# Four-layer conditional kernel on one core: layer 1 turned round, and the last queries moved behind the keys

## The chip, the cores and the metric

The kernel runs on one core of a Trainium2 chip. The metric is device time in microseconds (us), the median of several runs. Everything is fp32.

## The reference

`x` has 64 sequences of 64 tokens of width 512. Four layers follow, each with a residual. Which weights, adapter, cache window or subject matrix a sequence uses comes from small integer inputs.

```
x = x + x @ W0[id[b]] + b0[id[b]]                                  # layer 0: one of 16 matrices
x = x + x @ W1.T + s[ad[b]] * (x @ A[ad[b]].T) @ Bm[ad[b]].T       # layer 1: one of 8 rank-16 adapters
q, k, v = x @ Wq.T, x @ Wk.T, x @ Wv.T                             # layer 2: 8 query heads, 4 key heads of 64
q, k = rope(rms(q)), rope(rms(k)); new k, v go into a paged cache at kv_len[b] ...
x = x + softmax(mask(q k^T)) v @ Wo.T                              # window of 256 positions
x = x + out3,  out3[b] = W3[sub[b]]^T x[b] + side[sub[b]]          # layer 3: contracts over the tokens
```

## The kernel before

The 4096 tokens are 32 tiles of 128 (two sequences each), in groups of 1, 1, 2 and seven times 4 tiles. All instructions stand in an order written out by hand, for every engine. The first stage makes layers 0 and 1 and the queries, keys and values; the second makes attention and layer 3.

In the loop of the first stage, the steps of group g+1's layer 0 alternate with the queries and keys of group g, and after the steps stands layer 1 of group g+1.

- **Layer 0** (`layer0`, L479): p0 of one tile, two sequences side by side as two matmuls of 64 token columns each, every sequence with its own matrix W0 of 1 MB. ACT copies p0 to s0 (L484), TensorE turns it (`turn0`, L491), DVE adds it to x1 (L493), which POOL has filled with x plus the bias (`bias0`, L465). The matrices are loaded by SP two steps ahead (`load_pair0`, L455), four buffers.
- **Layer 1** (`layer1`): features on the partitions and tokens along the rows, a whole group at once. px (L501) is the product with all eight adapters' A (8 x 16 = 128 rows); DVE masks it with each sequence's own adapter and scaling to xa (L503). Then, for each of four blocks of 128 output features, ph is four matmuls with w1 (L512) and one with all eight adapters' B (L513), and DVE adds x1 to x2 (L514).
- **Keys and queries**: pk (L550) and pq (L563), then root mean square and rotation (`turned`, L524 to L544) on ACT, DVE and POOL. The query is turned (`turn_q`, L582), copied by ACT and stored to qTd; the new keys and values go to kvd (L557); `keep_x2` turns x2 back to tokens on the partitions (L573) and stores it to x2d.
- **Old keys** (`collect`, L228 to L237): 34 rounds of an indirect gather of 1 MB by POOL into one of three buffers `st` and a store of 1 MB to kvd by SP. From group 3 on, four rounds stand in each layer 1 and one in the third step.
- **Windows** (`windows`, L240 on): small DVE work that finds which rows of kvd each sequence reads; it is cut into pieces (`background`) that stand between the other work.

PSUM has three pools in the first stage: two banks for p0, two for pt, four for the rest. After the last layer 1 (group 9) stand the four key products of its tiles, then their four queries with the turns, then the second stage.

The second stage has its own PSUM pools, a ring of seven banks and one for the projection. Per tile: gathers of key and value rows from kvd by POOL (`load_kv`, L704), query and mask loads, key turns (L770, L776), scores (L789), softmax on DVE and ACT (L797, L801, L813), turns (L822, L826), attention (L836), projection (L859) and layer 3 (L871). The last tile's query stays in SBUF and is turned at the start of this stage (`turn_last`).

Of the kernel before, what the change touches and what calls it, by code (L numbers as in the profile page):

```python
# [23 lines left out]
E = 16  # L24
# [22 lines left out]
GROUPS = [128, 128, 256] + [512] * 7  # L47
NG = len(GROUPS)
T0 = [sum(GROUPS[:g]) for g in range(NG)]
TG = max(GROUPS)  # L50
# [9 lines left out]
def body(ctx: ExitStack, tc: tile.TileContext, a: dict, out: bass.AP):  # L60
# [10 lines left out]

    const = ctx.enter_context(tc.tile_pool(name="const", bufs=1))
# [10 lines left out]
    qlast = const.tile([128, H, HD], F32, name="qlast")  # L83

    wo_p = ctx.enter_context(tc.tile_pool(name="wo", bufs=1))
    wo = wo_p.tile([128, KC, D], F32, name="wo")
    with ExitStack() as pa:

        wp = pa.enter_context(tc.tile_pool(name="wp", bufs=4))
        xp = pa.enter_context(tc.tile_pool(name="xp", bufs=2))  # L90
        op = pa.enter_context(tc.tile_pool(name="op", bufs=3))
        x1p = pa.enter_context(tc.tile_pool(name="x1p", bufs=1))
        wts = pa.enter_context(tc.tile_pool(name="wts", bufs=1))
        su = pa.enter_context(tc.tile_pool(name="su", bufs=1))
        tt = pa.enter_context(tc.tile_pool(name="tt", bufs=1))
        wk = pa.enter_context(tc.tile_pool(name="wk", bufs=2))
        pl0 = pa.enter_context(tc.tile_pool(name="pl0", bufs=2, space=PSUM))
        pt0 = pa.enter_context(tc.tile_pool(name="pt0", bufs=2, space=PSUM))
        pmm = pa.enter_context(tc.tile_pool(name="pmm", bufs=4, space=PSUM))

        def mm(name):
            return pmm.tile([128, 512], F32, tag="mm", name=name)


        pa.enter_context(tc.manual_schedule(
            engines={getattr(mybir.EngineType, e) for e in ("PE", "DVE", "Activation", "Pool", "SP")}
        ))
# [9 lines left out]
        scal = su.tile([128, 1], F32, name="scal")  # L117
        nc.scalar.dma_start(scal, a["scal"])
        gain = su.tile([128, 2, 2, HALF], F32, name="gain")
# [12 lines left out]
        brow = x1p.tile([B, D], F32, name="brow", tag="xa")  # L132
# [5 lines left out]

        w1 = wts.tile([128, KC, D], F32, name="w1")
        aT = wts.tile([128, KC, NA * RANK], F32, name="aT")  # L140
        bmT = wts.tile([128, D], F32, name="bmT")
        wq = wts.tile([128, KC, D], F32, name="wq")
        wkv = wts.tile([128, KC, D], F32, name="wkv")

        def load_weight(t, name):
            nc.sync.dma_start(t, a[name].rearrange("(c p) f -> p c f", p=128))

# [10 lines left out]

        biasT = su.tile([128, KC, B], F32, name="biasT")
        pb = mm("pb")  # L160
        for c in range(KC):
            TE.transpose(pb[:, c * B : (c + 1) * B], brow[:, c * 128 : (c + 1) * 128], ident[:B, :B])
        S.copy(biasT.rearrange("p c b -> p (c b)"), pb[:, : KC * B])

        def scalars():
            V.tensor_scalar(p16, pidx, 4, None, ALU.logical_shift_right)
            V.tensor_copy(p16f, p16)

            V.tensor_scalar(amask, toki[:, 1, :], p16f, scal, ALU.is_equal, ALU.mult)

            V.tensor_scalar(gain, gain, 1.0, None, ALU.add)
            V.tensor_scalar(gain[:, 0], gain[:, 0], SCALE, None, ALU.mult)
            V.tensor_scalar(gsw[:, :, 0, :], gain[:, :, 1, :], -1.0, None, ALU.mult)
            V.tensor_copy(gsw[:, :, 1, :], gain[:, :, 0, :])
            V.memset(epst, EPS)
            V.tensor_tensor(eye2, ident[:, :64], ident[:, 64:], ALU.add)

        p16 = su.tile([128, 1], I32, name="p16")
        p16f = su.tile([128, 1], F32, name="p16f")
        amask = su.tile([128, B], F32, name="amask")  # L180
        gsw = su.tile([128, 2, 2, HALF], F32, name="gsw")
        epst = su.tile([128, 1], F32, name="epst")

        trig = {name: su.tile([128, NT, HALF], F32, name=name) for name in ("sin", "cos")}

        def rotation(lo):

            sh = [128, 8, HALF]
            hi = lo + 8
# [11 lines left out]
            for name, turn, shift in (("sin", 0.0, 0.0), ("cos", 0.25, 0.5 * PI)):  # L201
                ni = tmp("ni", I32)
# [3 lines left out]
                r = trig[name][:, lo:hi]  # L206
# [12 lines left out]

        quart = su.tile([128, JOLD, 2], I32, name="quart")  # L220

        def collect():

            rows, before = BLOCK // 4, None
            for j in range(JOLD):
                for q in range(2):
                    st = op.tile([128, rows * 2 * G * HD], F32, name="st")
                    P.indirect_dma_start(  # L228
                        out=st, out_offset=None, in_=a["kvc"].rearrange("(n r) d -> n (r d)", r=rows),
                        in_offset=bass.IndirectOffsetOnAxis(ap=quart[:, j, q : q + 1], axis=0),  # L230
                    )
                    if before:
                        nc.sync.dma_start(*before)
                    to = kvd[:OLD].rearrange("(p j q r) d -> p j q (r d)", p=128, q=2, r=rows)
                    before = (to[:, j, q], st)
                    yield
            nc.sync.dma_start(*before)  # L237


        def windows():  # L240
# [59 lines left out]

            ns = NW + 2
            diag = su.tile([B, B, ns], F32, name="diag")
# [6 lines left out]
            ps = mm("pst")  # L309
# [31 lines left out]
            valp = su.tile([128, BLOCK, hb, 2], F32, name="valp")  # L341
            cov = su.tile(sh, F32, name="cov")
            tok = su.tile(sh, F32, name="tok")
# [14 lines left out]
            hit = su.tile([128, BLOCK, 2 * hb], F32, name="hit")  # L358
# [58 lines left out]
            for c in range(3):  # L417
                yield
                po = mm("po")
# [15 lines left out]


        xs = {}

        def load_x(g):
            xs[g] = xp.tile([128, KC, TG], F32, name="xt")[:, :, : GROUPS[g]]  # L440
            nc.sync.dma_start(
                xs[g], a["xT"][:, T0[g] : T0[g] + GROUPS[g]].rearrange("(c p) t -> p c t", p=128)
            )

        x1s, x2s, p0s, qrs = {}, {}, {}, {}

        w0s = {}

        def load_pair0(g, k):

            ws = w0s[g, k] = []
            for b in range(T0[g] // T + 2 * k, T0[g] // T + 2 * k + 2):
                w = wp.tile([128, KC, D], F32, name="w")
                r = nc.sync.value_load(tok1[0:1, 0, b : b + 1], min_val=0, max_val=E - 1)
                nc.sync.dma_start(  # L455
                    w, a["W0"][bass.ds(r, 1)].rearrange("a (c p) o -> p (a c) o", p=128)
                )
                ws.append(w)

        def bias0(g):  # L460

            n = GROUPS[g]
            x1 = x1s[g] = x1p.tile([128, KC, TG], F32, name="x1")[:, :, :n]
            for c in range(KC):
                P.tensor_tensor(  # L465
                    x1[:, c, :].rearrange("p (b t) -> p b t", t=T),
                    xs[g][:, c, :].rearrange("p (b t) -> p b t", t=T),
                    bc(biasT[:, c, T0[g] // T : (T0[g] + n) // T, None], [128, n // T, T]),
                    ALU.add,
                )  # L470

        def layer0(g, k):

            ws, xt = w0s.pop((g, k)), xs[g]
            p0 = pl0.tile([128, D], F32, name="p0")
            for c in range(KC):
                for h in range(2):
                    b = 2 * k + h
                    TE.matmul(  # L479
                        p0[h * T : (h + 1) * T, :], xt[:, c, b * T : (b + 1) * T], ws[h][:, c, :],  # L480
                        start=c == 0, stop=c == KC - 1,
                    )
            s0 = x1p.tile([128, D], F32, name="s0", bufs=2)
            S.copy(s0, p0)  # L484
            p0s[g, k] = s0

        def turn0(g, k):
            s0, x1 = p0s.pop((g, k)), x1s[g]
            pt = pt0.tile([128, KC, 128], F32, name="pt")
            for c in range(KC):  # L490
                TE.transpose(pt[:, c, :], s0[:, c * 128 : (c + 1) * 128], ident)  # L491
            xk = x1[:, :, k * 128 : (k + 1) * 128]
            V.tensor_tensor(xk, pt, xk, ALU.add)  # L493

        def layer1(g):
            x1 = x1s.pop(g)
            n = GROUPS[g]
            gb = slice(T0[g] // T, (T0[g] + n) // T)
            px = mm("px")[:, :n]
            for c in range(KC):  # L500
                TE.matmul(px, aT[:, c, :], x1[:, c, :], start=c == 0, stop=c == KC - 1)  # L501
            xa = x1p.tile([128, TG], F32, name="xa")[:, :n]
            V.tensor_tensor(  # L503
                xa.rearrange("p (b t) -> p b t", t=T), px.rearrange("p (b t) -> p b t", t=T),
                bc(amask[:, gb, None], [128, n // T, T]), ALU.mult,
            )
            x2 = x2s[g] = x1p.tile([128, KC, TG], F32, name="x2")[:, :, :n]
            for oc in range(KC):
                ph = mm("ph")[:, :n]
# [468 lines left out]
```

## Time and profile before

| | |
|---|---|
| median of 3 runs | 993.87 us (993.85 to 994.07) |
| the profiled execution | 993.43 us, span 991.5 us |
| mean granted TensorE clock | 0.994 |
| DMA moved | 257.23 MB, mean 259 GB/s |
| first stage's last layer 1 ends | 549.5 us |
| first scores of the second tile start | 599.2 us |

The profile is of one execution. PE is TensorE, DVE VectorE, ACT ScalarE, POOL GpSimd, SP SyncE; "SPq" and "POOLq" are their queues, which issue DMAs. A group of instructions is named by line, engine and output<-input. The chain of waits follows the work that ended last back from the last instruction. "DMA share" is the mean busy share of 16 DMA engines in a stretch.

### The profile page before, as it was taken

The page shows a single profiled execution, that of the slowest core. Times are in us where ns is not written, and L with a number is a line of the kernel's source. Part 1 is how long each engine was busy: PE and PEld are TensorE (multiplying, and loading weights), DVE is VectorE, ACT ScalarE, POOL GpSimd, SP SyncE. Part 2 cuts the span into 40 slices and gives each one's busy share as a digit, 9 for nine tenths or more (in the row PEclk, how much of TensorE's full clock was granted, in tenths as well). Part 3 has the DMA queues.
Part 4 walks back from the last instruction along what each step waited for, and adds up shares of the span by engine and source line. Part 5 has one row for each costly group of instructions (what it writes and reads, how often), then busy time and mean ns, then how long its engine had stood idle before and what let it go on. Part 6 is the DMA issues. An engine that isn't in the chain of part 4 may idle for free.

```text
span 991.5 us, 16856 instructions
## 1 busy us (share of the span) xinstructions
PE 953.4 (96%) x5289; PEld 530.6 (54%) x5289; DVE 642.1 (65%) x1761; ACT 389.0 (39%) x1043; POOL 348.7 (35%) x463
## 2 busy tenths in 40 slices
PE   3989999999999999999999979999999999999997
PEld 1645444444444444444444446766666667776663
DVE  3664556647756766676474468777777777777772
ACT  1111224222122022032121247666666666666662
POOL 1122322333243333333322265444444444444400
PEclk9999999999999999999999999999999999999999
DMA  8954897988989979979957598566666666666611
GB/s 274 345 207 171 314 353 278 371 312 314 361 336 327 377 281 373 357 283 364 360 214 287 226 303 257 180 206 204 207 199 210 204 206 209 204 201 199 209 50 43
DMA packets 115115, 257.23 MB, mean 259 GB/s; under 512 B 22194, under 2 KB 32819, under 8 KB 106323
## 3 DMA queue, kind: packets, MB, share of 16 engines
q1 hardware_dynamic: 95874, 177.29, 49.7%
q0 software_dynamic: 17744, 77.74, 23.6%
q10 hardware_dynamic: 1408, 1.13, 0.4%
q8 instruction: 42, 0.69, 0.3%
q14 instruction: 47, 0.38, 0.1%
HBM read 186.62 MB, written 69.50 MB: 258 GB/s over the span
## 4 chain that ended last, share of the span: by engine, by line
PE 92%; DVE 4%; DMA 2%; ACT 1%; issue 0%; SPq 0%; ACTq 0%; DVEq 0%
PE py L859 12%; PE p L479 12%; PE pk L550 12%; PE pq L563 11%; PE ph L512 10%; PE po L836 8%; PE ps L789 7%; PE ppt L822 6%; PE ph L513 3%; PE pkt L770 2%; PE px L501 2%; PE pz L871 2%; PE pt L491 1%; PE ppt L826 1%; PE pkt L776 1%; PE pqt L582 1%
## 5 line engine op out<-in xcount | busy, mean ns | idle before, releaser
L704 POOL DMA_INDIRECT kv<-kvd,idxn x128 | 126.1, 985 | 184.5 <-PE po L836 138.6
L801 ACT ACTIVATE pr<-pr,mx 128x320 f32<-128x320 f32 x256 | 140.1, 549 | 25.0 <-DVE mx L797 25.0
L797 DVE CUSTOM_DVE_ANT_0 pr<-ps,mb 128x320 f32<-128x320 f32 x256 | 107.9, 487 | 33.6 <-PE ps L789 27.5
L479 PE MATMUL p<-w,xt 128*64 128x512 f32 x512 | 120.1, 608 | 0.1
L859 PE MATMUL py<-wo,oT 128*128 128x512 f32 x256 | 118.4, 605 | 1.6 <-DVE oT L854 0.8
L512 PE MATMUL ph<-x,w 128*128 128x512 f32 (+2 forms) x320 | 118.9, 515 | 0.0
L550 PE MATMUL pk<-wkv,x 128*128 128x512 f32 x256 | 117.5, 604 | 0.0
L563 PE MATMUL pq<-wq,x 128*128 128x512 f32 x256 | 115.2, 592 | 0.0
L484 ACT COPY s<-p 128x512 f32<-128x512 f32 x32 | 18.8, 586 | 187.2 <-PE p L479 187.1
L512 PEld LDWEIGHTS ph<-x,w 128*128 128x128 f32 x320 | 58.1, 196 | 55.2 <-issue 53.6
L813 DVE TENSOR_SCALAR pr<-pr,sm 128x320 f32<-128x320 f32 x256 | 85.1, 394 | 2.3
L550 PEld LDWEIGHTS pk<-wkv,x 128*128 128x128 f32 x256 | 46.3, 189 | 70.6 <-issue 64.7
L836 PE MATMUL po<-pT,kv 128*64 128x128 f32 (+1 forms) x1536 | 82.1, 278 | 0.0
L789 PE MATMUL ps<-kT,qT 64*128 64x320 f32 x512 | 78.7, 447 | 2.5 <-DMA qTd<-qT 2.5
L544 POOL TENSOR_TENSOR qr<-qn,sq 128x512 f32<-128x512 f32 x28 | 46.6, 1665 | 94.4 <-DVE qn L543 77.6
L859 PEld LDWEIGHTS py<-wo,oT 128*128 128x128 f32 x256 | 46.0, 189 | 62.7 <-issue 60.0
L836 PEld LDWEIGHTS po<-pT,kv 128*64 128x64 f32 (+1 forms) x1536 | 68.9, 135 | 19.9 <-DVE mx L797 13.6
L544 POOL TENSOR_TENSOR kvn<-qn,sq 128x256 f32<-128x256 f32 x32 | 23.3, 729 | 158.2 <-ACT kvn L556 132.3
L493 DVE TENSOR_TENSOR x<-pt,x 128x512 f32<-128x512 f32 x32 | 21.9, 691 | 81.2 <-PE pt L491 68.2
L479 PEld LDWEIGHTS p<-w,xt 128*64 128x64 f32 x512 | 35.0, 139 | 67.9 <-issue 65.6
L563 PEld LDWEIGHTS pq<-wq,x 128*128 128x128 f32 x256 | 46.2, 190 | 46.4 <-issue 46.2
L228 POOL DMA_INDIRECT st<-in_kvc,quart x34 | 33.9, 998 | 92.0 <-DMA kvd<-st 86.7
(176 smaller groups left out, 1387.1 us busy)
## 6 DMA issues: line engine op xcount, KB each, us to landing
w<-in_W SPq DMA_DIRECT2D x64, 1024.0 KB
kvd<-st SPq DMA_DIRECT2D x34, 1024.0 KB
kvd<-kvn SPq DMA_DIRECT2D x32, 256.0 KB
x2d<-x2n SPq DMA_DIRECT2D x32, 256.0 KB
x2r<-x2d SPq DMA_DIRECT2D x32, 256.0 KB
qTd<-qT SPq DMA_DIRECT2D x31, 256.0 KB
qT<-qTd SPq DMA_DIRECT2D x29, 256.0 KB
xt<-in_xT SPq DMA_DIRECT2D x7, 1024.0 KB
```

Of the source, the lines that this page charges most:

```text
L479: TE.matmul(p0[h * T : (h + 1) * T, :], xt[:, c, b * T : (b + 1) * T], ws[h][:, c, :], start=c == 0, stop=c == KC - 1,)
L512: TE.matmul(ph, w1[:, c, os_], x1[:, c, :], start=c == 0, stop=False)
L544: X.tensor_tensor(to, qn, t2, ALU.add)
L550: TE.matmul(pk, x2s[g][:, c, ts], wkv[:, c, :], start=c == 0, stop=c == KC - 1)
L563: TE.matmul(pq, x2s[g][:, c, ts], wq[:, c, :], start=c == 0, stop=c == KC - 1)
L704: P.indirect_dma_start(out=kv[:, n, :], out_offset=None, in_=kvd, in_offset=bass.IndirectOffsetOnAxis(ap=at, axis=0),)
L789: TE.matmul(ps[g2][:, :NPOS], qT[rows, gp, b2].rearrange("p h t -> p (h t)"), kT[rows, gp, b2 * NPOS : (b2 + 1) * NPOS], start=True, stop= ...
L797: V.tensor_tensor_reduce(out=p, in0=ps[g2][:, :NPOS], in1=mb[:, b2, :], scale=-1.0, scalar=3.0e38, op0=ALU.add, op1=ALU.min, accum_out=mx[ ...
L801: S.activation(p, p, AF.Exp, bias=mx[:, g, b2 : b2 + 1], scale=-1.0, accum_out=sm[:, g, b2 : b2 + 1],)
L813: V.tensor_scalar(p, p, sm[:, g, b2 : b2 + 1], None, ALU.mult)
L836: TE.matmul(po[b2][g2 * 64 : (g2 + 1) * 64, gp * 128 : (gp + 1) * 128], kv[rows, n, (G + g) * HD : (G + g + 1) * HD], pT[rows, c, m * 128 ...
L859: TE.matmul(py, oT[:, c].rearrange("p b t -> p (b t)"), wo[:, c, :], start=c == 0, stop=c == KC - 1)
```

## The change

Layer 1 holds tokens on the output partitions, as the other products do. For each tile, the weights loaded into TensorE are the tile's x1, the moving operand is w1, and p1 is a tile of 128 tokens by 512 features. Of the adapters, only the two that a tile needs are used. Their A (2 x 16 rows) is loaded per pair of sequences by SP (eight loads of 32 KB for four tiles) and their B is gathered per four tiles by POOL and scaled by DVE. Four tiles stand in the four column groups of 32 for A and in the four row groups of 32 for B. The residual is in w1, to which the identity is added once. ACT copies p1 to x2n, which is stored to x2d as it is and turned once for the products of layer 2.

x is loaded and kept in tiles, not groups, and the bias is added tile by tile. A query stands one step behind its keys. The queries of the last six tiles (26 to 31) stand behind the last layer 1: 26 before the last keys, 27 to 30 between the last keys and the first scores, 31 and the rest of 30 within the first two tiles of attention. Their rotation factors are made before. Old-key rounds are four in each layer 1 from group 3 on and two in the steps (first and second tile of a group). The mask table is made within the pieces of `windows`, and wo is loaded at the start of the second stage. One ring of seven PSUM banks and one for the projection serves both stages.

```diff
-GROUPS = [128, 128, 256] + [512] * 7
+GROUPS = [1, 1, 2] + [4] * 7
+LATE = 6
...
-        pl0 = pa.enter_context(tc.tile_pool(name="pl0", bufs=2, space=PSUM))
-        pt0 = pa.enter_context(tc.tile_pool(name="pt0", bufs=2, space=PSUM))
-        pmm = pa.enter_context(tc.tile_pool(name="pmm", bufs=4, space=PSUM))
+    ring = ctx.enter_context(tc.tile_pool(name="ring", bufs=7, space=PSUM))
+    pyp = ctx.enter_context(tc.tile_pool(name="pyp", bufs=1, space=PSUM))
...
+        def load_a(o):
+            ao = aos[o] = ab.tile([128, 4, 2 * RANK, KC], F32, name="ao")
+            for q in range(8):
+                b = 8 * o + q
+                r = nc.sync.value_load(tok1[0:1, 1, b : b + 1], min_val=0, max_val=NA - 1)
+                nc.sync.dma_start(
+                    ao[:, q // 2, q % 2 * RANK : (q % 2 + 1) * RANK].rearrange("p r c -> p (r c)"),
+                    a["aT"][bass.ds(r, 1)].rearrange("a p f -> p (a f)"),
+                )
...
+        def layer1(tiles):
+            o = tiles[0] // 4
+            ps = slice(32 * (tiles[0] % 4), 32 * (tiles[-1] % 4) + 32)
+            pxa = bank("pxa")
+            for c in range(KC):
+                for i in tiles:
+                    j = i % 4
+                    TE.matmul(pxa[32 * j : 32 * j + 32, :128], aos[o][:, j, :, c], x1s[i][:, c, :], ...)
+            xa = wk.tile([128, 2, T], F32, name="xa", bufs=2)
+            V.tensor_tensor(xa[ps], pxa[ps, :128]..., bc(own2[ps, :, None], ...), ALU.mult)
+            for i in tiles:
+                p1[i] = bank("p1")
+                for c in range(KC):
+                    TE.matmul(p1[i], x1s[i][:, c, :], w1[:, c, :], start=c == 0, stop=False)
+                if i > 3:
+                    next(bg, None)
+                    next(old, None)
+            for i in tiles:
+                js = slice(32 * (i % 4), 32 * (i % 4) + 32)
+                TE.matmul(p1[i], xa[js]..., bos[o][js, :D], start=False, stop=True)
+            for i in tiles:
+                x2n = x2ns[i] = wk.tile([128, D], F32, name="x2n", bufs=4)
+                S.copy(x2n, p1[i])
+                nc.sync.dma_start(x2d[i * 128 : (i + 1) * 128, :], x2n)
...
+            for k in range(m):
+                layer0(i0)
+                load_next(i0)
+                if i0 % 4 == 1 and i0 // 4 + 1 < NT // 4:
+                    load_a(i0 // 4 + 1)
+                    load_b(i0 // 4 + 1)
+                turn_x2(i)
+                pq = product(q, wq, "pq")          # q: the tile before i
+                turn0(i0)
+                run(parts_q(q, pq, P))
+                keep_kv(i, product(i, wkv, "pk"), P)
+                if i > 3 and i % 4 < 2:
+                    next(old, None)
+                turn_q(made.pop(0))                # the tile before q
...
+    for i in range(NT - LATE + 1, NT - 1):         # queries 27 to 30
+        pq = product(i, wq, "pq")
+        if i > NT - LATE + 2:
+            turn_q(i - 2)
+        parts[i] = parts_q(i, pq, V, cs[i])
...
+    keys(0)
```

## The prediction

> **What bounds the kernel now.** The page first: busy times and the chain that ended last.
>
> ```profile
> PE 953.4 (96%) x5289; PEld 530.6 (54%) x5289; DVE 642.1 (65%) x1761; ACT 389.0 (39%) x1043; POOL 348.7 (35%) x463
> ...
> PE 92%; DVE 4%; DMA 2%; ACT 1%; issue 0%; SPq 0%; ACTq 0%; DVEq 0%
> ```
>
> TensorE is the bound nearly everywhere, so PE work removed is time removed, unless something else becomes late. The chain in order of time shows one group of four token tiles (start, us, what; each fp32 matmul shows as two instructions, called passes here):
>
> ```profile
> 253.27 3.44 PE px L501 x8
> 256.71 3.43 PE ph L512 x8
> 260.14 0.86 PE ph L513 x2
> ...
> 273.87 3.58 PE p L479 x16
> 277.46 3.63 PE pk L550 x8
> 281.09 0.44 PE pt L491 x4
> 281.53 3.43 PE pq L563 x8
> ```
>
> Layer 1 lasts from 253.27 to 273.87, 20.60 us: px 3.44, then four times 3.43 + 0.86. The four steps after it take 11.96 each; the group repeats every 68.4. A pass over 512 columns is 0.429 us, a transpose 0.11.
>
> Next, the stretches (span, busy of PE, PEld, DVE, ACT, POOL, granted clock, DMA share, GB/s): two early ones, one layer 1, one whole group.
>
> ```profile
> 70.00:73.00 3.00, 0.95 (x2) 0.84 (x3) 1.89 (x9) 0.00 (x0) 0.00 (x0) 0.73 0.00 0
> 73.00:77.00 4.00, 4.00 (x11) 3.13 (x10) 0.43 (x1) 0.00 (x0) 0.00 (x0) 0.50 0.00 0
> ...
> 253.30:273.90 20.60, 20.60 (x50) 8.76 (x51) 15.18 (x18) 1.32 (x4) 5.23 (x5) 1.00 1.00 371
> 273.90:342.30 68.40, 68.40 (x226) 30.25 (x226) 44.98 (x73) 14.24 (x36) 25.30 (x33) 1.00 0.92 340
> ```
>
> DMA is the second bound: full in layer 1, 0.92 over a group. The timeline shows what each bound already costs (in brackets, the idle time before and its releaser):
>
> ```profile
> 72.05 1.22 PE L513 MATMUL ph<-xa,bmT 128*128 128x256 f32 x2 [3.54 <-DVE xa L503]
> ...
> 342.92 0.94 POOL L228 DMA_INDIRECT st<-in_kvc,quart  x1 [10.74 <-DMA kvd<-st]
> ```
>
> In an early group PE waits for xa, and after that wait runs at clock 0.50. POOL waits 10.7 us for a buffer of old keys, still unharmful.
>
> **Layer 1 on PE.** p1 is 4 matmuls a tile of the same pass: 4 x 3.43 = 13.72 a group. The A products become 16 matmuls of 32 weight columns, 32 passes over 128 tokens. The trace has none four column tiles abreast. Bounds: four quarter-passes of a transpose, 32 x 0.027 = 0.86; nothing abreast, 32 x 0.11 = 3.5. The nearest row has four quadrants abreast:
>
> ```profile
> L836 PE MATMUL po<-pT,kv 64*64 64x128 f32 x512 | 21.4, 282 | 0.0
> ...
> L871 PE MATMUL pz<-x,w 64*64 64x512 f32 x128 | 17.6, 592 | 0.0
> ```
>
> 21.4 / 512 = 42 ns a pass, so 32 x 42 = 1.34. The B products are 8 passes over 512 columns in four row tiles: bounds 8 x 0.107 = 0.86 and 8 x 0.429 = 3.43; the second row gives 137 ns a pass, 1.10. A change of tile shape: pk after the 64-wide p took 3.63 where pq took 3.43, so 0.2 each; three more a group, 0.6. Together 1.34 + 13.72 + 1.10 + 0.6 = 16.76 against 20.60: 3.84 saved, times seven groups 26.9. Ends: 15.44 a group (36 saved) and 21.25 (4.6 lost). The Trainium skill, "TensorEngine Tiling (Array Packing)", section Tiling Modes, says that changing the tiling mode drains TensorE, which speaks against this change; it gives no time, and the 0.2 us above is what the trace shows beside it.
>
> The residual moves into w1 (identity added once): 23 us leave DVE, and one x2 copy per tile (0.6) is added to ACT, 39% busy. Both are hidden under PE. The bias adds are the same POOL work in tile pieces (0.40 each, four a tile), the B scaling adds 8 short DVE operations; nothing of them ends last. x comes in tile pieces of the same bytes. wo is loaded behind the first masks and used by the first projection, two tiles (24 us) later; without that cover its 1 MB is 2.8 us.
>
> **The first three groups.** Gained: xa is now needed only after p1, 3.43 us or more later, so the waits of 2.3 (at 45.4) and 3.5 (at 72.0) go, and with them the half clock, about 2.6 by the stretches; the group of two tiles loses 1.2 of PE work. Lost: where one layer-0 tile is followed at once by its transposes (tiles 2, 4, 6) PE waits for the copy of s0, 0.7 each as at 22.6: 2.1. The eight A loads stand on SP behind w1, x and the second pair of W0, 3.4 MB; at 371 GB/s that is 9.2 us behind the first pair's landing at 16.4, so the first A product starts near 26.5, not 24.1: 2.5 (0 to 10, if the eight small issues themselves hold it). Net 5.9 + 2.6 + 1.2 - 2.1 - 2.5 = 5.1.
>
> **The turn to attention.** Before:
>
> ```profile
> 549.54 13.73 PE pk L550 x32
> ...
> 585.88 6.82 DMA mb<-maskd
> ...
> 599.22 2.35 PE ps L789 x16
> ```
>
> From 549.54 to 599.22 are 49.7 us with about 38 of PE work (4 pk, 4 pq, 9 sets of transposes of 0.43, two key sets, one score set, one turn): some 11.6 of waits, for queries, query and mask loads. Afterwards the keys come first; the last kvn goes out 3.6 us after the last pk, POOL's gathers start 2.8 later as at 570.0, take 6.4 to issue and some 2 to land, 15 in all, and the four products 27 to 30 (13.8) with two transposes (0.9) lie over just that. Masks and queries are issued in the meantime. What is left: 1.1 for the first x2 copy, 0.6 for the queries of tile 30, some 4.5 where normalising tile 0 now shares DVE with two queries. PE work 45.3 (two queries move here out of the loops, 6.9) plus 6.5 is 51.8; less the 6.9 that left the loops, 44.9: 4.8 gained. The shared PSUM ring of seven gives each bank back a full step (12 us) later in the loops, longer than any eviction; if evictions were late it would cost what they lag.
>
> **DMA.** Loads a group before: W0 8, x 1, key/value, x2, q stores 3, and five rounds of old keys (gather 1, store 1): 22 MiB, 23.1 MB; the row says 340 GB/s x 68.4 = 23.3. After: six rounds a group while they last (34 rounds, from layer 1 of group 3 to that of group 8) and 0.5 of adapters: 25.7 MB. PE's period would be 68.4 - 3.8 = 64.6; 340 / 0.92 = 370 GB/s makes 25.7 MB last 69.4. So for five groups DMA falls behind by 4.8 each, 24. W0 is issued two steps ahead (345.9 for use at 366.2) and needs 2.36 MB / 370 = 6.4 to land: 14 us of cover, used up once. Loss 24 - 14 = 10. Bounds: 0, if the full DMA carries a mix with more 8 KB rows faster, and 24, if queueing behind the stores eats the cover. SP also gets 8 adapter loads a group, each with a register load, in the second step: about 1.3 each by the pairs of w3 at 599 to 601, 10 us; it fits in the step, and queued behind it are a kvn store, an old-key store and the next W0, which still has its cover. The Trainium skill, "DMA: Bandwidth & Descriptors", section Specifications, sets 358 GB/s of HBM per core; the layer-1 stretch shows 371, so the measurement decides; by 358 the five groups would fall behind by 36 in place of 24, and the sum below would end at 979.
>
> **Sum.** The profiled run took 993.4 (span 991.5 and 1.9 around it), 0.4 under the median of 993.87. 26.9 + 5.1 + 4.8 - 10 = 26.8 off: 966.6, with the 0.4 put back 967.
>
> **Rivals.** (a) DMA hides: the loops run at 64.6, gain 36.8, 957; with both products at their lower ends 9 less, 948. For it: stores of 8 KB rows, and rounds throttled by POOL, not by W0. Against: share 1.00 in layer 1 already. (b) Slower: POOL is in order, and the bias adds of the next tile now stand in every step behind old-key gathers. The fourth gather of a layer 1 started 21.4 us after that layer's start (321.5 to 342.9); the bias then takes 1.6, and x1's add is due at 16.8 + 7.5 = 24.3. Behind it on DVE stand the queries' and keys' chains, behind those ACT's copy of the next s0, with about 4 us of spare. Every further us is PE's, in six groups; 36.8 / 6 = 6.1 a group turns the whole change into a loss, that is a fourth gather later than 24.3 + 4 + 6.1 - 1.6, +33. For it: DMA slows the very stores it waits for. Against: a slower queue also delays less than half of that, and three buffers stay. At +34.5 it costs 7.6 x 6 = 46, 9 over: 1003. (c) Nothing abreast: layer 1 at 21.25, then 4.6 lost in place of 26.9 gained, and no DMA deficit (period 69): 989. Against: L836 and L871 run abreast.
>
> **Chances.** Forecast with a DMA loss of 3 to 24: 0.50 (955 to 981). (a) 0.30. (b) 0.07. (c) 0.04. The rest, a mixture of lesser waits of POOL and DMA up to 990: 0.09. The range 946 to 985 takes (a) at its lower end and the forecast with the loss of 24 and some waits. Over 0.2% (2 us, about what a measurement of this kernel can tell from no change): faster 0.90, same 0.02, slower 0.08.
>
> **What would show it.** Right: in the chain, a layer 1 of 16 to 17.5 us, 13.7 of it p1; no wait for xa before 82 us and no clock of 0.50 there; DMA share near 1.00 over whole groups 4 to 8, with PE waits for W0 from the second of them on, a few us each; the turn with PE waits of 5 to 8. Wrong: groups of 64 to 65 us throughout (then (a)); PE waiting on s0 or x1 with POOL's bias behind a gather (then (b)); A products above 3 us a group (then (c)).

## The result, and the profile after

The changed kernel takes 1023.61 us (1020.42 to 1025.50) beside 993.86 for the kernel before: 1.0299 times as long, 95% interval 1.0269 to 1.0329. The forecast was 967, range 946 to 985, with 0.90 on faster. Its sign was wrong.

Page after, busy times and the chain by engine:

```profile
PE 944.3 (92%) x5385; PEld 510.5 (50%) x5385; DVE 613.1 (60%) x1736; ACT 414.5 (41%) x1082; POOL 374.7 (37%) x566
...
PE 59%; DMA 7%; DVE 2%; ACT 1%; SPq 1%; issue 1%; POOL 0%; DVEq 0%; ACTq 0%; POOLq 0%
```

TensorE's busy time fell by 9 us, but its share of the span went from 96% to 92%: PE now waits. The timeline of one group on PE (start, us, instructions, idle before and releaser) has the new layer 1 and the new wait:

```profile
274.91 1.11 PE L625 MATMUL pxa<-x,ao 128*32 128x128 f32 x32
275.95 14.00 PE L638 MATMUL p<-w,x 128*128 128x512 f32 x32
289.88 1.14 PE L646 MATMUL p<-bo,xa 32*128 32x512 f32 x8
290.95 3.65 PE L233 MATMUL p<-w,xt 128*64 128x512 f32 x16
...
319.22 1.94 PE L233 MATMUL p<-w,xt 128*64 128x512 f32 x2 [4.37 <-DMA w<-in_W]
321.74 5.37 PE L233 MATMUL p<-w,xt 128*64 128x512 f32 x14 [0.58 <-DMA w<-in_W]
```

Layer 1 lasts 16.04 us (274.91 to 290.95) where it lasted 20.60: the saving is there. Two steps later PE waits 5 us for W0, and the passes after it are slow (14 in 5.37 us, where 16 take 3.65). All waits of PE, the largest (in all, times, longest):

```profile
PE p L233 <- DMA w<-in_W: 36.5, 9, 11.8
PE pst L488 <- DVE ones L485: 11.7, 1, 11.7
PE pt L257 <- ACT s L236: 6.0, 7, 2.9
PE p L646 <- DVE xa L630: 4.8, 2, 2.5
```

Of the first, 13.3 us lie at the very start (first loads of all); 23.2 lie between layer 1 of group 4 and that of group 9.

Where the time went, by the starts of layer 1 in both traces (profiled runs; the forecast column spreads its 26.8 us over the stretches as its text does):

| stretch | before | forecast | after | after less forecast |
|---|---|---|---|---|
| start to layer 1 of group 3 | 113.8 | 108.7 | 117.7 | +9.1 |
| layer 1 of group 3 to that of 4 | 69.2 | 65.3 | 82.2 | +16.8 |
| groups 4 to 8 (four periods) | 275.5 | 270.1 | 290.0 | +19.9 |
| layer 1 of group 8 to that of 9 | 70.2 | 59.5 | 65.2 | +5.8 |
| from there to the second scores | 70.6 | 68.8 | 73.8 | +5.0 |
| rest of attention | 392.3 | 392.3 | 394.2 | +1.9 |
| span | 991.5 | 964.7 | 1023.1 | +58.4 |

### The profile page after: what moved, and what is told of

Its sections match the earlier page's. It is cut to its first block, busy times and chain, and to the rows that moved or that the text cites. A ratio compares the mean times of both kernels' runs of the same rounds, so it can differ in the third digit from the quotient of the medians.

```text
span 1023.1 us, 17633 instructions
## 1 busy us (share of the span) xinstructions
PE 944.3 (92%) x5385; PEld 510.5 (50%) x5385; DVE 613.1 (60%) x1736; ACT 414.5 (41%) x1082; POOL 374.7 (37%) x566
## 4 chain that ended last, share of the span: by engine, by line
PE 59%; DMA 7%; DVE 2%; ACT 1%; SPq 1%; issue 1%; POOL 0%; DVEq 0%; ACTq 0%; POOLq 0%
PE py L895 11%; PE po L872 8%; PE ps L825 7%; PE p L638 5%; PE ppt L858 5%; PE p L233 5%; PE pq L138 5%; PE pk L138 4%; DMA w<-in_W 4%; PE pkt L806 2%; PE pz L907 1%; PE ppt L862 1%; PE pkt L812 1%; DMA qTd<-qTs 1%; DMA st<-in_kvc,quart 1%
## 5 line engine op out<-in xcount | busy, mean ns | idle before, releaser
L233 PE MATMUL p<-w,xt 128*64 128x512 f32 x512 | 141.3, 669 | 36.7 <-DMA w<-in_W 36.5
L638 PE MATMUL p<-w,x 128*128 128x512 f32 x256 | 116.0, 610 | 0.0
L138 PE MATMUL pk<-wkv,x 128*128 128x512 f32 x256 | 115.2, 594 | 0.6 <-ACT x L659 0.6
L133 POOL TENSOR_TENSOR qr<-qn,sq 128x512 f32<-128x512 f32 x27 | 34.6, 1283 | 217.1 <-DVE qn L132 211.0
L233 PEld LDWEIGHTS p<-w,xt 128*64 128x64 f32 x512 | 39.5, 152 | 121.3 <-issue 80.9
L638 PEld LDWEIGHTS p<-w,x 128*128 128x128 f32 x256 | 49.0, 195 | 61.1 <-issue 60.4
L872 PEld LDWEIGHTS po<-pT,kv 128*64 128x64 f32 (+1 forms) x1536 | 68.9, 135 | 19.9 <-DVE mx L833 13.6
L651 ACT COPY x2n<-p 128x512 f32<-128x512 f32 x32 | 16.6, 598 | 120.7 <-PE p L646 120.7
L858 PE MATMUL ppt<-ident,pr 128*128 128x128 f32 x512 | 62.2, 273 | 3.1 <-DVE pr L849 3.1
```

The lines of the kernel that those rows point to most:

```text
L138: TE.matmul(ps, x2s[i][:, c, :], w[:, c, :], start=c == 0, stop=c == KC - 1)
L233: TE.matmul(p0[hs, :], xs[i][:, c, hs], w0s[i][h][:, c, :], start=c == 0, stop=c == KC - 1)
L638: TE.matmul(p1[i], x1s[i][:, c, :], w1[:, c, :], start=c == 0, stop=False)
L858: TE.transpose(pt[:, n * 128 : (n + 1) * 128], pr[:, g, at : at + 128], ident)
L872: TE.matmul(po[b2][g2 * 64 : (g2 + 1) * 64, gp * 128 : (gp + 1) * 128], kv[rows, n, (G + g) * HD : (G + g + 1) * HD], pT[rows, c, m * 128 ...
```

## The experiments

Theories, as the expectations name them. T1: loads and stores start late, because they stand in order in queues behind others, SP's above all. T2: the DMA engines have no room in groups 4 to 8, with six rounds of old keys a group in place of five. T3, formed later: the four rounds bunched in layer 1 fill DMA, whatever the queue. All are edits of the changed kernel; some diffs show only what differs from an earlier run, and cuts in them are marked with three dots. A "period" is the time from one group's layer 1 to the next. The first four ran on a chip where the kernel before takes 994 us, the others on chips where it takes 1012: in their traces the attention behind the second scores lasts 410 to 412 us where it lasts 393 to 394 on the first chip. So ratios to the kernel before are compared (0.001 is 1 us), and differences between kernels of different chips are read together with the periods of the traces.

**1. The mask in its own buffer.**

```diff
-            um = su.tile([128, NM], F32, name="um", tag="big")
+            um = su.tile([128, NM], F32, name="um")
```

> Base: the changed kernel, 1023.6 us. The mask um gets a buffer of its own, so that diag no longer waits for the store of um. In the changed kernel's layer 1 of group 3 PE waits 11.71 us at pst (L488) and then runs at half clock. T1 (late starts in queues): the wait and its clock go, minus 12 to 17 us, about 1009; layer 1 of that group 16 to 20 us in place of 32. T2 (the DMA engines have no room in groups 4 to 8): group 3 gets shorter by the same wait, but the loads it had time to fetch during it come later, so at most minus 6, about 1018.

Measured 1.0153 (1.0088 to 1.0218), 14.5 us less than the changed kernel, as T1 expected; from layer 1 of group 3 to the next now 69.8 in place of 82.2, so 12.3 us of it lie where the edit acts. Timelines of SP, DVE and PE in the changed kernel show the wait that went:

```profile
130.84 0.34 SPq L476 DMA_DIRECT2D maskd<-um  x1
...
140.24 0.62 DVE L481 TENSOR_TENSOR diag<-ident,stat 64x448 f32<-64x448 f32 x1 [9.46 <-DMA maskd<-um]
...
141.05 1.86 PE L488 MATMUL pst<-diag,ones 64*128 64x448 f32 x2 [11.71 <-DVE ones L485]
```

The mask table um and diag share a buffer. The store of um is issued at 130.84, after three gathers of old keys of 1 MB each (POOL, 126.9 to 131.1), while the DMA engines are full (share 0.97 from 128.40 to 141.05). So DVE gets the buffer 9.46 us late, and PE, in order, stands at a windows product between two p1 products. The kernel before stored the mask at 36.8, from a buffer of its own. The stretches after the wait (the last three numbers are granted clock, DMA share and GB/s):

```profile
141.05:143.00 1.95, 1.95 (x3) 0.66 (x3) 0.06 (x1) 0.00 (x0) 0.00 (x0) 0.50 1.03 437
143.00:145.00 2.00, 2.00 (x3) 0.97 (x4) 1.85 (x10) 0.00 (x0) 1.79 (x4) 0.50 1.00 422
145.00:147.00 2.00, 2.00 (x3) 0.71 (x3) 0.72 (x3) 0.00 (x0) 1.22 (x4) 0.50 1.04 381
147.00:149.00 2.00, 2.00 (x8) 0.64 (x7) 0.00 (x0) 0.00 (x0) 0.00 (x0) 0.81 0.72 279
```

This wait is paid twice: some 6.7 us at clock 0.50 follow, 3.4 us more. Not every wait is: `um_own` still waits 2.17 us at the same product, and there the clock stays at 1.00.

**2. Adapter loads spread**, two in each step in place of eight in one.

```diff
-                    load_a(i0 // 4 + 1)
                     load_b(i0 // 4 + 1)
...
+                if i0 // 4 + 1 < NT // 4:
+                    load_a(i0 // 4 + 1, range(0 if i0 == 1 else 2 * (i0 % 4), 2 * (i0 % 4) + 2))
```

> Base: the changed kernel, 1023.6 us. Two adapter loads in each layer-0 step in place of eight in one. In the changed kernel those eight hold SP for 14.76 us (319.64 to 334.4) and the next W0 is issued at 338.7. T1 (late starts in SP's queue): the second PE wait for W0 of each group (0.6 to 6.8 us, with half clock behind it) shrinks; minus 8, about 1015. T2 (no room in the DMA engines): the bytes of a group stay the same, 0 plus or minus 2, about 1023.

Measured 1.0291 (1.0252 to 1.0331): nothing that can be told. The eight loads hold SP for 14.8 us, and they are not what matters.

**3. Old keys spread**: two rounds in layer 1 and one in every step, still six.

```diff
-                    next(old, None)
+                    if i % 4 < 2:
+                        next(old, None)
...
-                    if i > 3 and i % 4 < 2:
+                    if i > 3:
```

> Base: the changed kernel, 1023.6 us. The six rounds of old keys of each group: two in layer 1 and one in every step, in place of four in layer 1 and one in two of the steps. T1 (late starts): SP's stores in layer 1 wait for two gathers fewer (each 3 to 6 us), the W0 of the first step is issued about 10 us earlier and POOL's bias of that step as well; minus 15, about 1008. T2 (no room in the DMA engines): six rounds a group still, the same bytes: 0 plus or minus 3, about 1023.

Measured 1.0065 (1.0043 to 1.0087), 23 us less: T1's direction, more than it expected, and against T2. The edit moves POOL's gathers and the bursts of bytes as well as SP's stores; run 10 moves SP's order alone.

**4. W0 through ACT's queue.**

```diff
-                nc.sync.dma_start(
+                q.dma_start(
                     w, a["W0"][bass.ds(r, 1)].rearrange("a (c p) o -> p (a c) o", p=128)
...
-                load_next(i0)
+                if i is not None:
+                    turn_x2(i)
+                load_next(i0, nc.scalar)
...
-                if i is not None:
-                    turn_x2(i)
```

> Base: the changed kernel, 1023.6 us. From the first group on, W0 is loaded through ACT's DMA queue, right behind ACT's copy of x2, in place of SP's; so no old-key store, x2d store or adapter load stands ahead of it. T1 (late starts in SP's queue): PE's waits for W0 (36.5 us in 9 stretches, the longest 11.8) and the half clock behind them go: minus 25 to 40, about 990. T2 (no room in the DMA engines): the loads start earlier but end when the bytes are through; minus 10 or less, about 1014.

Measured 1.0279 (1.0243 to 1.0314): almost nothing, so against T1 as put. In the group of the second fence above, ACT's timeline has the loads 11.5 us earlier than SP's had them (308.44), and later ones that hold ACT:

```profile
296.89 1.59 ACTq L216 DMA_DIRECT2D w<-in_W  x2
...
310.76 3.04 ACTq L216 DMA_DIRECT2D w<-in_W  x2
...
318.88 5.35 PE L233 MATMUL p<-w,xt 128*64 128x512 f32 x16 [3.84 <-issue]
```

PE still started that tile only at 318.88, 22 us after the issue; from SP's queue it was 13.3 (308.44 to 321.74, second fence). The trace names no releaser for this wait. In the 22 us the DMA engines were full (share 0.99, then 1.04), with rounds of old keys under way. So an earlier issue alone did not help; that the bytes under way held the load back fits, but is not shown. PE's waits for ACT's copy of s0 rose from 6.0 to 12.0 us. The Trainium skill, "DMA: Bandwidth & Descriptors", section "Issuing engines are not separate DMA queues", says that a second issuing engine saves only sequencer time, usually small beside the DMA, since all share the same 16 DMA engines. This run agrees: 11.5 us of earlier issue were not had back. That the sequencer's time is small does not hold here: the four x2d stores of that group hold SP for 4.24 us (run 10), where their 1.05 MB at the 372 GB/s of its layer 1 would take an estimated 2.8.

**5 to 8. Five rounds, and combinations.** First (five): as 3, but no round in the fourth step.

```diff
-                    if i > 3:
+                    if i > 3 and i % 4 < 3:
```

> Base: the kernel with two old-key rounds in layer 1 and one in every step (1001.8 us, periods of groups 5 to 8 68.5, 69.5, 65.9 and 70.5). Here the fourth step of a group has no round: five rounds a group, as in the kernel before, so 2.1 MB less a group (one gather and one store of 1.05 MB), 5.6 us of DMA at 375 GB/s. T2 (the DMA engines have no room in groups 4 to 8): each of these groups falls to the larger of 63 us of DMA and 64.6 us of PE, so 64.6 to 66.5; minus 3 a group, minus 10 to 16 in all, about 989. T1 (late starts in SP's queue): layer 1 and its two rounds are the same, so 0 plus or minus 4, about 1001.

Measured 0.9955 (0.9927 to 0.9983), 11 us under 3. The four periods of groups 4 to 8 average 64.8 us (63.7, 66.3, 65.3, 64.0) after 68.6 in 3. So T2 holds for this part: once the order is better, six rounds cost 3.8 us a group.

Mask buffer and spread together (um_spread):

> Base: the changed kernel, 1023.6 us; both edits that helped: the mask in its own buffer (1006.1 alone) and two old-key rounds in layer 1 with one in every step (1001.8 alone). T1 (two separate late starts): they add up, minus 39, about 985. T2 (the DMA engines have no room in groups 4 to 8): the group of the mask gains its 12 to 17 us, but the old-key rounds of the later groups stand no earlier against DMA, so groups of 69 each remain: about 990.

Measured 0.9988 (0.9961 to 1.0016): less gain than either theory had (T2's 990 would be 0.996, the end of the interval); the two edits do not add up, and with six rounds three of the four periods are again over 68 us (68.4, 65.3, 70.8, 68.6).

Mask buffer, five rounds, and `qTs` with `bufs=4` (um_five):

> Base: the changed kernel, 1023.6 us. The mask in its own buffer, five old-key rounds a group (two in layer 1, three in steps), and four buffers for the turned queries qTs in place of two. T2 (the DMA engines have no room with six rounds a group): groups 4 to 8 at 64.6 to 66.5, the turn to attention 4 us shorter for the buffers of qTs; about 970. T1 (late starts alone): as with six rounds, and the turn: about 981. Faster than the kernel before (994) in both.

Measured 0.9826 (0.9796 to 0.9857); 0.983 x 994 is 977, between the two. It beats the kernel before. In addition W0 on ACT's queue (um_five_w):

> The mask in its own buffer, five old-key rounds a group, four buffers for qTs, and in addition W0 loaded through ACT's queue behind its copy of x2. With room in the DMA engines, T1 (late starts) expects the last waits for W0 to go: minus 8 against the same kernel with W0 on SP's queue, about 965 to 970. T2 (no room was the cause): 0 plus or minus 3 against it.

Measured 1.0057 (1.0027 to 1.0087): 23 us worse. PE's waits for s0 rise from 6.3 to 16.4 us, 10 of the 23 us: the loads stand in ACT's own order, among its copies. What makes the rest is not shown.

**9. The order 4 + 1 with five rounds.** `um_five`, whose order is 2 + 3 (two rounds in layer 1, three in steps), with four rounds in layer 1 and one in the first step.

```diff
-                    if i % 4 < 2:
-                        next(old, None)
+                    next(old, None)
...
-                    if i > 3 and i % 4 < 3:
+                    if i > 3 and i % 4 < 1:
```

> Against the kernel with the mask in its own buffer, four qTs buffers and five old-key rounds a group, two in layer 1 and three in steps (ratio to the kernel before 0.983): the same five rounds, but four in layer 1 and one in the first step, as SP's queue had them in the changed kernel. T2 (six rounds were too many bytes): with five there is room, so the order is worth 0 to 4 us, ratio 0.983 to 0.987. T1 (the four rounds in layer 1 hold SP and with it the next W0): 2 to 4 us in each of five groups, 10 to 20 us, ratio 0.993 to 1.003.

Measured 1.0129 (1.0067 to 1.0192), 30 us over the order 2 + 3 with the same bytes, more than T1 itself expected. This tells order from bytes, though not yet whose order: POOL's gathers move too. One whole group of 4 + 1, and one of 2 + 3, in one stretch each (span; busy of PE, PEld, DVE, ACT, POOL; clock, DMA share, GB/s):

```profile
331.82:402.98 71.16, 67.25 (x249) 29.12 (x249) 39.52 (x75) 19.40 (x44) 27.02 (x46) 0.95 0.92 331
```

```profile
314.49:379.62 65.13, 64.77 (x250) 28.55 (x249) 39.98 (x75) 19.39 (x44) 27.64 (x46) 1.00 0.96 357
```

4 + 1 is 6 us longer while DMA has 8% to spare over the group: its bytes are not its bound. SP's waits at the old-key store (for the gather before it) and at W0 (for PE to free the buffers), first in the kernel before, then in 4 + 1, then in 2 + 3:

```profile
SPq L233 <- DMA st<-in_kvc,quart: 113.2, 25, 10.3
...
SPq L455 <- PE p L479: 50.4, 14, 16.8
```

```profile
SPq L401 <- DMA st<-in_kvc,quart: 112.8, 20, 9.3
...
SPq L216 <- PE p L233: 10.7, 7, 2.6
```

```profile
SPq L401 <- DMA st<-in_kvc,quart: 27.2, 8, 7.1
...
SPq L216 <- PE p L233: 8.7, 5, 2.7
```

Before the change SP waited as long for the gathers, but still came to W0 (L455) early and waited there for PE, 50.4 us in all. In 4 + 1 it waits only 10.7 at W0 (L216): the cover is gone. In 2 + 3 it waits no longer, 8.7, yet PE hardly waits: its waits for W0 are 15.3 us in all, most of them at the first loads, and 35.5 in 4 + 1. So a short wait of SP says that the load has no slack, and not that it is late.

**10. x2d stores behind the next W0** (`keep_x2` issues them), bytes and rounds unchanged: on 9, and alone on the changed kernel.

```diff
-                nc.sync.dma_start(x2d[i * 128 : (i + 1) * 128, :], x2n)
+                stores.append((x2d[i * 128 : (i + 1) * 128, :], x2n))
...
                 load_next(i0)
+                keep_x2()
```

> Against the kernel with five rounds a group, four in layer 1 and one in the first step (1.013): the four x2d stores of layer 1 stand behind the next W0 loads on SP's queue in place of ahead of them. Bytes and rounds are unchanged. There SP had W0 to issue from 351.5 on (PE done with the buffers) and reached it at 363.7, of which 4.1 us for the x2d stores; PE then waited 3.9 us and ran at half clock. T1 (SP's order): W0 4 us earlier, most of the waits go, 3 to 6 us in each of six groups, 18 to 36 in all, ratio 0.977 to 0.995. T3 (the burst of bytes in DMA is what delays W0): 0 plus or minus 5 us, ratio 1.008 to 1.018.

> The changed kernel (1.030) with that edit alone: x2d stores behind the next W0 loads. T1 (SP's order): W0 4.2 us earlier where it was issued 14 us late; with six rounds a group the DMA engines still bound a group at 68 to 69 in place of 71 to 75, so 10 to 16 us less, ratio 1.014 to 1.020. T3 (burst of bytes): 0 plus or minus 3, ratio 1.027 to 1.033.

Measured 0.9935 (0.9896 to 0.9973), 19 us under 9; and 1.0178 (1.0142 to 1.0215), 12 us under the changed kernel. Both are in T1's range and out of T3's: four stores that stood ahead of a load on an in-order queue cost some 12 to 19 us. PE's waits for W0 fall with them, from 35.5 us to 23.4 and from 36.5 to 27.5. One W0 pair in 9, then with the stores behind it, from SP's issue to PE's start on the second matrix:

```profile
363.70 1.62 SPq L216 DMA_DIRECT2D w<-in_W  x2
376.68 6.12 PE L233 MATMUL p<-w,xt 128*64 128x512 f32 x14 [3.91 <-DMA w<-in_W]
```

```profile
352.96 2.57 SPq L216 DMA_DIRECT2D w<-in_W  x2
366.54 5.34 PE L233 MATMUL p<-w,xt 128*64 128x512 f32 x14 [2.19 <-DMA w<-in_W]
```

That takes 13.0 and 13.6 us, so the load is not faster without the stores' bytes ahead of it. It is issued sooner: 29.6 us after the start of layer 1 (323.41) in place of 31.9 (331.82). SP in the kernel before, in the group of the prediction's first chain, and in the changed kernel, in the group of the first timeline:

```profile
256.85 16.60 SPq L233 DMA_DIRECT2D kvd<-st  x4
...
277.48 1.60 SPq L455 DMA_DIRECT2D w<-in_W  x2
```

```profile
281.06 21.27 SPq L401 DMA_DIRECT2D kvd<-st  x4
302.42 4.24 SPq L652 DMA_DIRECT2D x2d<-x2n  x4
...
308.44 1.74 SPq L216 DMA_DIRECT2D w<-in_W  x2
```

Before, the old-key stores took SP 16.6 us and were over before layer 1 was (273.87); W0 went out as soon as PE freed the buffers (277.46). Now they take 21.3 us, layer 1 is over at 290.95, and the x2d stores stand behind them: PE was done with the buffers at 294.6 and SP came to them at 308.44.

**11. The last rounds, the qTs buffers, the order on DVE.** All eight calls of group 3 make a round, so that none is left for the turn to attention:

> Against the same kernel (0.983): all eight calls of group 3 make a round of old keys (its DMA share is 0.81), five in each later group, so the last old-key store is issued in the last layer 1 and none in the turn to attention. If the turn (64 us there from the end of layer 1 to the second scores, with PE waits of 6.5, 2.2 and 1.6 us for key gathers) waits for those last stores: minus 6 to 12 us, ratio 0.971 to 0.977. If the turn is held by its own chain of keys, queries and masks: 0 plus or minus 2, ratio 0.983.

Measured 0.9829 (0.9803 to 0.9856): 0 against `um_five`. From the last layer 1 to the end it is 5 us shorter (484.8 after 490.1), but the first of the four periods is 3.5 longer. With two buffers for qTs:

> The kernel with eight calls in group 3, but with two buffers for qTs, as in the changed kernel, where ACT waited 5.2 us in the turn for a store out of them. If that wait is on the path: 3 to 5 us more than with four buffers. If the turn waits for something else: 0 plus or minus 2 us.

Measured 0.9838 (0.9809 to 0.9867): nothing that can be told; the wait of 5.2 us on ACT was not the bound. With the windows piece of a group's last step behind the xa multiply:

```diff
-                    other(i)
+                    if k == m - 1:
+                        held.append(i)
+                    else:
+                        other(i)
...
+            while held:                # in layer1, behind the xa multiply
+                other(held.pop())
```

> The kernel with eight calls in group 3, and in addition the windows piece (and the rotation piece) of the last step of a group emitted behind layer 1's xa multiply in place of ahead of it. In the changed kernel DVE reaches xa 2.3 and 2.5 us late in groups 1 and 2, after 3 us of such pieces, and PE runs at clock 0.50 for a while after. If those waits cost what the trace says, with the slow clock: 5 to 8 us less. If DVE then is late for something else in layer 1 (the sum of turn0): 0 plus or minus 2.

Measured 0.9735 (0.9712 to 0.9758), 9 us less, a little more than expected; layer 1 of group 3 starts at 107.6 in place of 114.6 (112.7 to 120.6 in all runs without this edit). This is the fastest kernel: 0.9735 x 993.9 is 967.5 us. That this is the forecast's 967 is chance: it is another kernel, with five rounds a group, and its stretches differ from the forecast's. The step that went, on DVE and PE of the changed kernel:

```profile
76.65 0.61 DVE L290 TENSOR_SCALAR bo<-bo 128x512 f32<-128x512 f32 x1
77.29 0.29 DVE L630 TENSOR_TENSOR xa<-pxa,own 64x128 f32<-64x128 f32 x1
...
77.64 1.13 PE L646 MATMUL p<-bo,xa 32*128 32x512 f32 x4 [2.54 <-DVE xa L630]
```

Ahead of these two on DVE stood the key chain and 3 us of windows pieces.

**12. Not abreast, and all together.** On that fastest kernel, the low-rank products of the third and fourth tile each behind their own main products:

> Against the best kernel so far (mask in its own buffer, four qTs buffers, two rounds in layer 1 and three in steps, windows pieces behind xa: 0.9735): the low-rank products of tiles 2 and 3 of a group follow their own tile's main products, so no four stand abreast (the first two tiles still pair up). By the trace of the changed kernel four abreast take 1.07 us for eight passes, and before the change two passes alone took 1.02. So 2.0 to 3.0 us more in each of seven groups, 14 to 21 us, ratio 0.988 to 0.994. If DMA bounds these groups (64 to 66 us, share 0.97), the product times hide and it is 0 plus or minus 3.

Measured 0.9859 (0.9839 to 0.9879), 12 us slower; periods 66.2 where they were 63.7. The products of B are where it goes:

```profile
320.11 1.13 PE L652 MATMUL p<-bo,xa 32*128 32x512 f32 x4
...
324.80 1.12 PE L652 MATMUL p<-bo,xa 32*128 32x512 f32 x2
```

Two passes last as long as four, and as eight do abreast (1.07 us from start to start): 2.1 us more a group, and 0.4 more for p1, whose products are now split by them. So four abreast are worth their 2.5 us in a group that PE bounds.

Rounds two in each layer 1 (four in the last), three or four in the steps, and x2d stores behind W0:

> The causes found, together: as the best kernel so far (0.9735), x2d stores behind the next W0 loads, and of the rounds of old keys two in each layer 1 (four in the last) and three or four in the steps, in place of eight in group 3. Group 4 took 70.2 there and 63.7 where group 3 had fewer rounds. T1: minus 4 to 8 us, ratio 0.966 to 0.970. If the last rounds in the last layer 1 hold up the turn to attention instead: 0 plus or minus 3, 0.971 to 0.977.

Measured 0.9749 (0.9725 to 0.9774): no gain over 0.9735. The four periods of groups 4 to 8 are 4 us shorter in all, and the stretch from layer 1 of group 3 is 5 us longer (74.6 after 69.6). Two things changed at once, so what the x2d stores alone bring there is not shown.

## Why the prediction was wrong

- **Layer 1 on PE: right.** Forecast 16.76, measured 16.04: pxa 1.04 (1.34), p1 13.93 (13.72), the B products 1.07 (1.10). Rival (c) is out: eight passes abreast took 1.07, and putting them apart cost 12 us.
- **DMA and SP: the step that failed.** "W0 is issued two steps ahead ..., 14 us of cover" took the issue time of the trace before, and "it fits in the step" looked at the adapter loads alone. The adapter loads were indeed harmless (a_spread), but the cover was gone. Layer 1 ends 4.6 us sooner, so W0 is needed sooner; the four stores that wait for gathers keep SP 21.3 us where they took 16.6; and the four x2d stores, moved to the end of layer 1, now stand between them and W0. In the group of the first timeline W0 is issued at 308.44, 6.4 us before PE is ready for it (314.85), and from the issue to PE's start on the second matrix it takes 13.3; the forecast had 20.3 and 6.4. The forecast costed bytes and not the position on the queue: queueing behind the stores was only its upper bound, a loss of 24. The four periods alone lost 29.9, that is 19.9 more than the 10 allowed. The stretch behind them (5.8 over) has W0 waits too and falls from 65.2 to 60.8 with the x2d stores moved. How much of the rest is SP's order, and how much the full DMA engines that run 4 met, was not separated. The deficit of bytes that it did cost is real once the order is mended: "25.7 MB last 69.4" against 68.6 measured with six spread rounds, and five spread rounds give 64.8, the 64.6 of PE alone.
- **The mask: no step at all.** The section on the change names it (made within the pieces of `windows`), and the prediction did not price it: 16.8 us over forecast in that group, 12.3 of it shown by the trace of um_own.
- **The first three groups.** "xa is now needed only after p1 ..., so the waits ... go" looked at PE's side alone. DVE reaches xa later too, at 77.29. Waits of 2.31 and 2.54 us and the half clock stayed; reordering DVE brought 9 us, 7.0 of them in this stretch, and layer 1 of group 3 then starts at 107.6, forecast 108.7. The A loads cost less than forecast: the first A product starts at 24.89, not near 26.5.
- **The turn.** 5.0 us over forecast, and 5.6 by the forecast's terms as written, which add to some 51.2 and not 51.8. The buffers of qTs were not the cause, and old-key rounds moved out of it brought 5 us only where there were some left. What bounds it stays open.
- **Rival (b)** had the right kind of mechanism, an in-order queue behind old-key gathers, but PE waited for SP's W0 and not for x1. POOL's fourth gather of that group started at 297.31, 22.4 us after layer 1's start, and DVE waited 6.3 us for the bias behind it. The chain of waits goes on from there over DVE and ACT to SP's x2d store at 306.29; its releasers are inferred, and whether a late bias holds SP too was not tried.

## What to carry to other kernels

When a stage gets shorter, look at who used its length as cover: list what each in-order queue does in it, and ask whether the next critical load is still issued on time. Before a change of order, look at the queue's own waits: an engine that waits at a load for its buffer has slack there (50.4 us in the kernel before); one that hardly waits has none, and whether its load is late depends on the way from issue to use (13 us here) against the time left. A moved side job, a mask or a table, is a step with a price as well, above all if its buffer is shared.

## What the hardware showed

- After a wait of PE of 11.7 us the clock stood at 0.50 until about 147.8, 6.7 us after PE resumed. After the wait of 2.54 us (at 77.64) half clock lasted some 3.4 us: the stretches 79 to 81 and 81 to 83 have clocks 0.62 and 0.53, that is 1.5 and 1.9 us at 0.50. The Trainium skill, "TensorE: Matmul & The Clock Gate", Part 1, gives at least one busy window of about 3.4 us before full speed; the short wait agrees with one, and the long one took twice that.
- DMA in short stretches moved 437 GB/s at share 1.03 and over whole groups at share 0.99 it moved 363 GB/s in the changed kernel and 383 with the rounds spread, so a full share is not one rate; which mix of transfers makes the difference was not measured.
- ACT as the second issuer of loads cost 23 us where hardly any load was late (um_five_w).
- Products of 32 rows and 512 columns took 1.05 us for two passes on one row tile, 1.06 for four on two tiles (run 12) and 1.07 for eight on four tiles (the changed kernel).
